# Moving the narrow t1 products of a two-layer graph kernel from behind the first attention unit to the front of the joined product

## The chip, the cores and the metric

The kernel runs on one core of one Trainium2 chip. The metric is the time of one execution on the device in microseconds (us), smaller being better. All data is 32-bit floating point.

## What is computed

Two layers run over 16 batch elements of 1024 nodes with 256 channels. Layer 0 weights the shared adjacency by a likeness of nodes, derives queries from it, and does attention with 4 heads; layer 1 is a pair of graph convolutions with the same adjacency. The core of the reference:

```
def layer0(x, para, adj, kv_w):          # x: 16 x 1024 x 256
    fea = transpose(x, (0, 2, 1))
    c_adj = mean(fea, axis=1)
    diff = c_adj[:, None, :] - c_adj[:, :, None]
    A = abs(abs(sigmoid(diff) - 0.5) - 0.5) * 2.0
    Wg = adj[None] * (A + transpose(A, (0, 2, 1))) * 0.5
    g = relu(einsum('bcn,bnm->bcm', fea, Wg) * para.reshape(1, C, N))
    q = heads(transpose(g, (0, 2, 1)))
    k, v = heads(x @ kv_w)
    attn = softmax(einsum('bhnd,bhmd->bhnm', q, k) * scale)
    return merge(einsum('bhnm,bhmd->bhnd', attn, v))

def graph_conv(x, adj, w_loop, w_neigh, b):
    return x @ w_loop + einsum('nm,bmh->bnh', adj, x @ w_neigh) + b

x = layernorm(x + layer0(x, para, adj, kv_w))
h = relu(graph_conv(x, adj, w1_loop, w1_neigh, b1))      # 256 -> 128
h = relu(graph_conv(h, adj, w2_loop, w2_neigh, b2))      # 128 -> 256
x = layernorm(x + (x + h) * 0.5)
```

`t1` in the kernel is `x @ w1_neigh` of the first convolution, a 1024 x 128 array.

## The kernel before

The batch elements are software-pipelined. While element b is in attention, the next element's query weights, keys and values are prepared (`q`, `kv`), the first convolution of element b-1 (`c1`) and the second convolution of element b-2 (`c2`) are done together, and element b-3 (`c3`) gets its last normalization.

**Attention in four units.** `UNITS` are four pairs of (heads, half of the queries). For each unit u, `Attention.scores(u)` (L618) makes 8 score tiles with products on half of TensorE's rows (64 x 128 weights, two products side by side, L626); ACT takes the exponential of each (L629) and VectorE sums them up (L633, L635), transposes the sum (L637) and reduces it (L640). `Attention.outputs(u)` (L643) multiplies the exponentials with the values, on half of TensorE's columns (L648), and VectorE transposes the result (L653). Between units the main loop (L1095 to L1122) calls one of three functions: `gap0` behind unit 0, `gap1` behind unit 1, `gap2` behind unit 2. `gap0` and `gap1` run for b = 1 to 14; `both`, the joined product, exists from b = 2 on.

**The t1 products.** `GraphConv.inner` (L750) makes t1 with 16 products of 128 columns (L755) into a PSUM tile of two banks and has ACT copy it to SBUF (L758, 128 x 1024). The group has 32 entries in a trace for each call: every 32-bit product is recorded as two passes.

**The joined product.** The first convolution of b-1 and the second of b-2 both multiply by the adjacency. `Joined` treats the pair as one blocked product with 7 in place of 8 block products (a Strassen form). Its left-hand sums of t1 and of the second convolution's h1 are made by `Joined.left` (L924) with four 128 x 512 additions, on GpSimd within the loop and on VectorE at the very end. Its right-hand sums of the adjacency lie in DRAM and are fetched by `Joined.fetch` (L920, DMA at L183). `Joined.run` (L942) starts with the loop products of `c1` (`GraphConv.loop`, L760; they use x and not t1), then takes products 1, 2, 6, 7, 5, 4 and 3 through `Joined.product` (L935), each of 4 products of 512 columns. Products 1 and 2 use t1 itself as weights; 6 uses `s12[:, 1]`, 7 `s34[:, 0]`, 5 `s12[:, 0]`, 3 `s34[:, 1]` and 4 h1. Into this sequence `gap1` hangs other work: the GpSimd sums for the next query (`FastQueries.left`, L534, behind product 1), the accumulation of the attention (`att.add`, L655, behind product 2), the likenesses (L490, L491), the last normalization of `c3` and more. The last batch element (L1178 to L1189) and the end of the kernel (L1191 to L1205) have their own order, in which `c1.inner()` and `both.left(...)` stand directly ahead of `both.run(...)`.

**What sets the order.** The whole program is under a manual schedule: each engine runs its instructions in the order of the Python calls, and waits are put in from the data dependencies and the buffers. SBUF rows (`row_tile`) come from a ring of 25 buffers, taken in the order of first use; a tile waits for the last readers of the tile 25 places earlier. PSUM has a ring of three two-bank tiles (`big_psum`, `half_psum`), which serves the scores, t1, the joined product's sums and the second convolution's outputs (`h2_ps`, L838, read by VectorE at L830), and a ring of two single banks. SyncE (SP) issues all DMAs of the loop in program order.

Of the kernel before, what the change touches and what calls it, by code (L numbers as in the profile page):

```python
# [18 lines left out]
def kernel(  # L19
# [31 lines left out]
    nc = tc.nc  # L51
# [47 lines left out]
    def row_tile(name):  # L99
        return work.tile([P, N], F32, tag="row", name=name, bufs=ROWS)  # L100
# [85 lines left out]
    def store(n, rows):  # L186
        for h in range(2):
            nc.sync.dma_start(out=far_adj[n][h], in_=rows[h])
# [7 lines left out]
    def adj_sums(rows01, k):  # L196

        w11, w21, w22 = (half_adj[ij][:, k, :] for ij in ((0, 0), (1, 0), (1, 1)))
        w12 = of_rows(rows01, k)
        t13, t24 = (row_tile(f"adjT_{n}_{k}") for n in (13, 24))  # L200
        t = {1: t13[:, 0:FB], 3: t13[:, FB:N], 2: t24[:, 0:FB], 4: t24[:, FB:N]}
        nc.vector.tensor_sub(t[1], w12, w11)
        nc.vector.tensor_sub(t[3], w22, w12)
        nc.vector.tensor_sub(t[2], w22, t[1])
        nc.vector.tensor_sub(t[4], w21, t[2])
        for n in t:
            nc.sync.dma_start(out=far_adj[n][k // 2][:, ts(k % 2, FB)], in_=t[n])
# [9 lines left out]
    def channel_major(blocked, name):  # L217

        dst = work.tile([P, NC, N], F32, tag="xT", name=name, bufs=2)
        for cc in range(NC):  # L220
            nc.vector.transpose(dst[:, cc, :], blocked[cc])
        return dst
# [35 lines left out]
    def means(q, xb, name):  # L258

        c_col = small.tile([P, NT], F32, tag="c_col", name=f"c_col_{name}", bufs=2)  # L260
        for t in range(NT):
            nc.scalar.activation(xb[:, t, :], xb[:, t, :], AF.Identity, accum_out=c_col[:, t:t + 1])
        nc.gpsimd.tensor_scalar_mul(c_col, c_col, 1.0 / C)
        line = dram.tile([1, N], F32, tag="line", name=f"line_{name}")
        nc.sync.dma_start(out=line.rearrange("o (t p) -> p (o t)", p=P), in_=c_col)
        q.c_col = c_col

        def row():
            q.c_row = work.tile([P, N], F32, tag="c_row", name=f"c_row_{name}")
            nc.sync.dma_start(out=q.c_row, in_=line.to_broadcast([P, N]))  # L270

        return row
# [241 lines left out]
    class FastQueries(Queries):  # L514
# [19 lines left out]
        def left(self, eng):  # L534
            s12, s34 = (row_tile(f"S_{self.b}_{k}").rearrange("p (s t c) -> p s t c", s=2, c=P) for k in range(2))
            eng.tensor_add(s12[:, 0], self.block(1, 0), self.block(1, 1))
            eng.tensor_sub(s12[:, 1], s12[:, 0], self.block(0, 0))
            eng.tensor_sub(s34[:, 0], self.block(0, 0), self.block(1, 0))
            eng.tensor_sub(s34[:, 1], self.block(0, 1), s12[:, 1])
            self.S = [s12[:, 0], s12[:, 1], s34[:, 0], s34[:, 1]]  # L540
# [366 lines left out]
    class Joined:  # L907
# [16 lines left out]
        def left(self, eng):  # L924

            t1 = [self.c1.t1[:, j * TJ:(j + 1) * TJ, :] for j in range(2)]
            h1 = [self.c2.h1[:, ts(j, FB)].rearrange("p (t f) -> p t f", f=HID) for j in range(2)]
            s12, s34 = (row_tile(f"R_{self.b}_{k}").rearrange("p (s t f) -> p s t f", s=2, f=HID) for k in range(2))
            eng.tensor_add(s12[:, 0], h1[0], h1[1])
            eng.tensor_sub(s34[:, 0], t1[0], h1[0])  # L930
            eng.tensor_sub(s12[:, 1], s12[:, 0], t1[0])
            eng.tensor_sub(s34[:, 1], t1[1], s12[:, 1])
            self.x = {1: t1[0], 2: t1[1], 3: s34[:, 1], 4: h1[1], 5: s12[:, 0], 6: s12[:, 1], 7: s34[:, 0]}

# [45 lines left out]
    def run():  # L980
# [57 lines left out]
        for b in range(B):  # L1038
            more = b + 1 < B
            att = Attention(b, xB, qT, kT, v)  # L1040
            c1, c2, c3 = (convs.get(b - k) for k in (1, 2, 3))
            both = Joined(c1, c2) if c2 else None
# [9 lines left out]

            def gap0():
                row = means(q, xb, str(b + 1))
                c1.inner()
                if both:
                    c2.load_x()
                    both.fetch(2, 3)
                    both.left(nc.gpsimd)
                row()  # L1060
                ready["xT"] = channel_major(blocked, f"xT_{b + 1}")

            def weigh_first():
                q.times_adj(0)
                q.times_adj(TJ)
                q.right(0)

            def gap1():
                for t in (0, TJ):
                    q.load(t)  # L1070
                if both:
                    both.fetch(1, 4)
                    both.run({1: (lambda: q.left(nc.gpsimd),),
                              2: (lambda: att.add(0, 1),),
                              6: (lambda: q.likeness(0), lambda: c3 and c3.moments()),
                              7: (lambda: q.likeness(TJ),),
                              5: (weigh_first,),
                              4: (lambda: c3 and c3.finish(out[b - 3]),),
                              3: (c1.turn_blocks,)})
                else:  # L1080
                    q.left(nc.gpsimd)
                    for t in (0, TJ):
                        q.likeness(t)
                    store("01", rows01)
                    c1.first(rows01, lambda: (att.add(1), adj_sums(rows01, 1), adj_sums(rows01, 2), weigh_first()))
                    c1.turn_blocks()

            def gap2():
                if both:
                    c2.last()  # L1090

            between = [gap0, gap1, gap2] if c1 and more else []
            if more:
                q = (FastQueries if c1 else Queries)(b + 1, xb)
# [96 lines left out]
        c1, c2, c3, c4 = (convs[B - k] for k in (1, 2, 3, 4))  # L1191
        both = Joined(c1, c2)
# [83 lines left out]
```

## Time and profile before

| | us |
|---|---|
| median of 3 runs | 2154.06 (2153.91 to 2154.83) |
| the profiled execution | 2154.23 |
| its span, first to last instruction | 2152.5 |
| t1 products, L755, busy in all 16 calls | 61.3 |
| t1 copies, L758, ACT, in all 16 calls | 16.2 |
| R sums, L929 to L932, GpSimd, 14 calls each | 21.7, 21.3, 21.7, 29.4 |

The granted TensorE clock was 0.998 over the span. How to read the page: "PE" is TensorE's products, "PEld" its loads of weights, "DVE" VectorE, "POOL" GpSimd; a line such as L755 is the line of the program that issued an instruction. In a timeline, each row gives the start of a group in us from the span's start, its length, the engine, the line, the operation, output and inputs, the shapes, and the number of instructions merged; in brackets stands the idle time of the engine ahead of it and what ended it. A pair such as 64\*128 or 128\*64 in the shapes is the part of the array that a product uses.

### The profile page before, as it was taken

The numbers are of one execution on the slowest core, as the hardware profiler recorded it, in microseconds if no ns is written. First come the engines' busy times: TensorE is split into PE (matmuls) and PEld (weight loads), VectorE is DVE, ScalarE is ACT, GpSimd is POOL, SyncE is SP. The second block draws the span as 40 slices with busy tenths as digits, with TensorE's granted clock in tenths as the row PEclk, the third lists the DMA queues.
The fourth block names the chain that finished last, engine by engine and source line by source line (L and its number), as shares of the span: only waits on it lengthen the run. The fifth ranks groups of instructions, "written<-read, shape, count | busy, mean of one in ns | idle before, by whom it ended". The sixth has DMA issues, their size and how long they took to land.

```text
span 2152.5 us, 23740 instructions
## 1 busy us (share of the span) xinstructions
PE 2138.9 (99%) x8360; PEld 1023.1 (48%) x8360; DVE 1905.3 (89%) x2350; ACT 1039.9 (48%) x1374; POOL 361.1 (17%) x201
## 2 busy tenths in 40 slices
PE   9999999999999999999999999999999999999998
PEld 5344444544445444454545445454454444544354
DVE  5999998899998999989999899999999899899964
ACT  4744545545345454455544555445553445545412
POOL 1011130211303113030120302203021130211021
PEclk9999999999999999999999999999999999999999
DMA  9493563736557365572755627555374563734343
GB/s 231 120 150 117 141 163 108 142 122 131 143 140 168 93 134 158 135 171 89 122 165 129 161 89 121 173 127 157 108 114 160 128 157 119 130 133 95 121 137 100
DMA packets 612207, 290.73 MB, mean 135 GB/s; under 512 B 504816, under 2 KB 569712, under 8 KB 612080
## 3 DMA queue, kind: packets, MB, share of 16 engines
q1 hardware_dynamic: 611808, 288.87, 55.7%
q8 instruction: 68, 1.11, 0.2%
q14 instruction: 59, 0.48, 0.1%
q10 hardware_dynamic: 272, 0.26, 0.0%
HBM read 242.35 MB, written 46.72 MB: 134 GB/s over the span
## 4 chain that ended last, share of the span: by engine, by line


## 5 line engine op out<-in xcount | busy, mean ns | idle before, releaser
L629 ACT ACTIVATE pr<-s 128x1024 f32<-128x1024 f32 x512 | 476.1, 1054 | 175.1 <-PE s L626 174.3
L635 DVE TENSOR_TENSOR acc<-acc,pr 128x1024 f32<-128x1024 f32 x384 | 492.7, 1283 | 42.2 <-DVE acc L635 2.4
L626 PE MATMUL s<-qT,kT 64*128 64x512 f32 x2048 | 456.8, 596 | 0.0
L648 PE MATMUL av<-pr,v 128*64 128x512 f32 x2048 | 453.6, 596 | 0.0
L626 PEld LDWEIGHTS s<-qT,kT 64*128 64x128 f32 x2048 | 191.7, 186 | 236.6 <-ACT pr L629 112.3
L328 POOL TENSOR_TENSOR rstd<-rstd,neg_half 128x32 f32<-128x32 f32 x16 | 98.9, 6182 | 1113.8 <-DVE rstd L326 1113.8
L648 PEld LDWEIGHTS av<-pr,v 128*64 128x64 f32 x2048 | 141.4, 137 | 298.6 <-issue 292.1
L490 ACT ACTIVATE wg<-c_row,c_col 128x1024 f32<-128x1024 f32 x128 | 146.1, 1141 | 76.4 <-DVE accB L637 65.7
L496 DVE SCALAR_TENSOR_TENSOR wg<-wg,adj 128x1024 f32<-128x1024 f32 x128 | 150.0, 1210 | 11.4 <-ACT wg L491 11.1
L939 PE MATMUL hu_ps<-adj,R 128*128 128x512 f32 x360 | 158.0, 595 | 0.0
L491 ACT ACTIVATE wg<-wg 128x1024 f32<-128x1024 f32 x128 | 135.3, 1057 | 4.1
L577 PE MATMUL g_ps<-wg,S 128*128 128x512 f32 x224 | 115.6, 598 | 0.0
L577 PE MATMUL g_ps<-T,S 128*128 128x512 f32 x224 | 115.2, 596 | 0.0
L577 PE MATMUL g_ps<-wg,x 128*128 128x512 f32 x224 | 109.0, 599 | 0.0
L633 DVE TENSOR_TENSOR acc<-pr,pr 128x1024 f32<-128x1024 f32 x64 | 80.5, 1258 | 30.0 <-ACT pr L629 30.0
L939 PE MATMUL hu_ps<-adjT,t 128*128 128x512 f32 x240 | 105.7, 593 | 0.0
L939 PEld LDWEIGHTS hu_ps<-adj,R 128*128 128x128 f32 x360 | 67.4, 190 | 78.8 <-issue 77.2
L586 ACT COPY P<-g_ps 128x512 f32<-128x512 f32 x14 | 8.2, 585 | 174.8 <-PE g_ps L577 174.8
L637 DVE STREAM_TRANSPOSE accB<-acc 128x1024 f32<-128x1024 f32 x64 | 79.7, 1245 | 2.2
L955 ACT COPY snap<-hu_ps 128x512 f32<-128x512 f32 x15 | 8.8, 585 | 150.3 <-PE hu_ps L939 150.3
L640 DVE TENSOR_REDUCE den_part<-accB 128x32 f32<-128x1024 f32 x64 | 78.1, 1220 | 2.2
L823 PE MATMUL h_ps<-w2n_sb,uT 128*128 128x256 f32 x240 | 72.8, 385 | 0.0
(204 smaller groups left out, 3020.6 us busy)
## 6 DMA issues: line engine op xcount, KB each, us to landing
adj<-in_adj_dram SPq DMA_DIRECT2D x128, 512.0 KB, 5.0
adj<-adjT SPq DMA_DIRECT2D x120, 512.0 KB, 10.1
para<-in_L_gnn_para_dram SPq DMA_DIRECT2D x32, 512.0 KB, 4.5
xB_a<-in_x_dram SPq DMA_DIRECT2D x128, 128.0 KB, 3.9
x1d<-xB_a SPq DMA_DIRECT2D x128, 128.0 KB, 3.4
x<-x1d SPq DMA_DIRECT2D x16, 1024.0 KB, 16.1
xB<-in_x_dram SPq DMA_DIRECT2D x120, 128.0 KB, 4.7
x<-in_x_dram SPq DMA_DIRECT2D x15, 1024.0 KB, 6.5
```

Of the source, the lines that this page charges most:

```text
L328: nc.gpsimd.tensor_tensor(self.rstd, self.rstd, neg_half, ALU.pow)
L490: nc.scalar.activation(wg, self.c_row, AF.Abs, bias=self.c_col[:, t:t + 1], scale=-1.0)
L491: nc.scalar.activation(wg, wg, AF.Tanh, scale=-0.5)
L496: nc.vector.scalar_tensor_tensor(wg, wg, 1.0, self.adj.pop(t), op0=ALU.add, op1=ALU.mult)
L577: nc.tensor.matmul(self.p[n], x_n[:, k, :], w_n, start=(k == 0), stop=(k == TJ - 1))
L626: nc.tensor.matmul(ps[:, ts(s, FB)], self.kT[rows, pair, ts(mt, P)], self.qT[rows, pair, ts(j, FB)], start=True, stop=True)
L629: nc.scalar.activation(pr, ps, AF.Exp)
L633: nc.vector.tensor_add(acc, self.pr[0], pr)
L635: nc.vector.tensor_add(acc, acc, pr)
L637: nc.vector.transpose(accB, acc)
L648: nc.tensor.matmul(pav[s * HD:(s + 1) * HD, :], self.v[:, mt, pair * P + s * HD:pair * P + (s + 1) * HD], self.pr[mt][:, ts(s, FB)], start ...
L939: nc.tensor.matmul(dst, self.x[n][:, k, :], half_adj[w][:, k, :] if w else of_rows(rows, k), start=(start and k == 0), stop=(k == TJ - 1), ...
```

## The change

In `gap0`, the call of `c1.inner()` and the four sums of `both.left(nc.gpsimd)` are taken out. In `gap1`, `c1.inner()` is put behind the two adjacency loads and, where there is a joined product, `both.left(nc.gpsimd)` behind it, both ahead of the fetch of adjacency sums 1 and 4 and of `both.run`. In b = 1, which has no joined product, `c1.inner()` then stands ahead of `q.left(nc.gpsimd)`, the likenesses and `c1.first`. In `Joined.left` the second and third of the four sums change places, so that `s12[:, 1]` is made ahead of `s34[:, 0]`; this holds wherever the helper is used.

```
             eng.tensor_add(s12[:, 0], h1[0], h1[1])
+            eng.tensor_sub(s12[:, 1], s12[:, 0], t1[0])
             eng.tensor_sub(s34[:, 0], t1[0], h1[0])
-            eng.tensor_sub(s12[:, 1], s12[:, 0], t1[0])
             eng.tensor_sub(s34[:, 1], t1[1], s12[:, 1])
...
             def gap0():
                 row = means(q, xb, str(b + 1))
-                c1.inner()
                 if both:
                     c2.load_x()
                     both.fetch(2, 3)
-                    both.left(nc.gpsimd)
                 row()
                 ready["xT"] = channel_major(blocked, f"xT_{b + 1}")
...
             def gap1():
                 for t in (0, TJ):
                     q.load(t)
+                c1.inner()
                 if both:
+                    both.left(nc.gpsimd)
                     both.fetch(1, 4)
                     both.run({1: (lambda: q.left(nc.gpsimd),),
```

The number of instructions of each engine's arithmetic is the same before and after: TensorE runs scores of unit 1 directly behind outputs of unit 0, and t1 between outputs of unit 1 and the loop products; ACT runs the t1 copy behind unit 1's exponentials in place of ahead of them; GpSimd keeps its order apart from the swap, and SyncE keeps its order of DMAs.

More of the change, by code (lines that the diff above doesn't have):

```diff
@@ L929, in left @@
             eng.tensor_add(s12[:, 0], h1[0], h1[1])
+            eng.tensor_sub(s12[:, 1], s12[:, 0], t1[0])
             eng.tensor_sub(s34[:, 0], t1[0], h1[0])
-            eng.tensor_sub(s12[:, 1], s12[:, 0], t1[0])
             eng.tensor_sub(s34[:, 1], t1[1], s12[:, 1])
@@ L1054, in gap0 @@
                 row = means(q, xb, str(b + 1))
-                c1.inner()
                 if both:
@@ L1058, in gap0 @@
                     both.fetch(2, 3)
-                    both.left(nc.gpsimd)
                 row()
@@ L1070, in gap1 @@
                     q.load(t)
+                c1.inner()
                 if both:
+                    both.left(nc.gpsimd)
                     both.fetch(1, 4)
```

## The prediction

> **What bounds the kernel now.** I read the busy times first, then TensorE's timeline around the place of the edit, then the same stretch on the other engines.
>
> ```profile
> PE   2138.9 (99%) x8360; PEld 1023.1 (48%) x8360; DVE 1905.3 (89%) x2350; ACT 1039.9 (48%) x1374; POOL 361.1 (17%) x201
> ```
>
> TensorE (PE) is busy for 2138.9 of 2152.5 us. A busy share can hide stalls, so I checked the starts: the loop products that open a joined product (L762) start 132.34 us apart in every batch element from the second joined one on (561.26, then 693.60; 958.28, then 1090.63). An interval that repeats this exactly waits for nothing; the time is the sum of TensorE's own blocks. A change can only shorten a block, or bring in a wait that is not there now.
>
> The blocks around the edit, from TensorE's timeline (start, length, group). Lengths include the pipeline's tail, so I use differences of starts.
>
> ```profile
> 1065.76 7.09 PE L648 MATMUL av<-pr,v 128*64 128x512 f32 x32
> 1072.77 3.84 PE L755 MATMUL t_ps<-w1n_sb,x1T 128*128 128x128 f32 x32
> 1076.54 7.14 PE L626 MATMUL s<-qT,kT 64*128 64x512 f32 x32
> 1083.61 7.09 PE L648 MATMUL av<-pr,v 128*64 128x512 f32 x32
> 1090.63 1.98 PE L762 MATMUL hu_ps<-x1T,w1l_sb 128*128 128x512 f32 x4
> 1092.45 7.03 PE L939 MATMUL hu_ps<-adjT,t 128*128 128x512 f32 x16
> ```
>
> The reader should see four changes of array shape: 128*64 (outputs) to the full array (t1), to 64*128 (scores), to 128*64, to the full array (loop). Steps: outputs 7.01, t1 3.77, scores 7.07, outputs 7.02, loop 1.82.
>
> The new order is already in the trace, at the last batch element, where the inner product stands right before the joined one, and where scores follow outputs with nothing between:
>
> ```profile
> 1992.14 7.09 PE L648 MATMUL av<-pr,v 128*64 128x512 f32 x32
> 1999.16 7.14 PE L626 MATMUL s<-qT,kT 64*128 64x512 f32 x32
> 2006.23 0.41 PE L662 MATMUL den_ps<-den_part,fold 128*128 128x32 f32 x2
> ...
> 2042.43 3.84 PE L755 MATMUL t_ps<-w1n_sb,x1T 128*128 128x128 f32 x32
> 2046.11 1.88 PE L762 MATMUL hu_ps<-x1T,w1l_sb 128*128 128x512 f32 x4
> 2047.83 3.60 PE L939 MATMUL hu_ps<-adjT,t 128*128 128x512 f32 x8
> ```
>
> Here outputs to scores is 7.02, scores 7.07, t1 followed by loop 3.68, loop after t1 1.72.
>
> **What the Trainium skill says.** "TensorEngine Tiling (Array Packing)", Tiling Modes, Key Properties: "Changing tiling mode (not just tile) drains the TensorE". It gives no price; the trace agrees and prices it: the same loop block is 1.82 behind outputs and 1.72 behind t1. "TensorE: Matmul & The Clock Gate", Step-by-step: the weights of a coming product are loaded while the present one runs. The weight loads of L762 and L939 agree (each starts some 0.43 ahead of its product). "SBUF — State Buffer", Who interferes with whom: a VectorE instruction with two SBUF inputs and a GpSimd instruction that reads SBUF exclude each other. The trace agrees: L387 of VectorE takes 1.75 beside GpSimd's S sums, while L386, of the same shape, takes 0.68.
>
> **The change part by part.**
>
> *TensorE.* No product is added or removed; 16 t1 products (32 recorded passes) move in 14 batch elements (b = 1 to 14; the last element and the ending have the order already). Per element:
> - t1 is followed by the full-array loop in place of scores: 3.77 − 3.68 = 0.09 saved.
> - The loop follows t1 in place of outputs: 1.82 − 1.72 = 0.10 saved.
> - Outputs to scores without t1 between: 7.02 against 7.01, and scores then take 7.07 as before: nothing.
> - Scores to outputs stays: nothing.
>
> Sum 0.19 us by 14 = 2.7 us, all on the path, since TensorE is the path. Two changes of shape fall away of four. The saving's own bounds are rounding of starts: 0.18 to 0.20 by 14, so 2.5 to 2.8.
>
> *ACT.* The t1 copy (L758, 1.01) moves from before the eight exponentials of unit 1 to behind them. They now follow the means (L262), which end at about 1070.45, before scores could start at 1072.8. So neither delays scores, and the copy finds ACT idle: ACT's exponentials end about 8.6 after their scores start, while outputs end 14.1 after. Cover on the new side: product 1 needs t1's copy for its weights, and only the loop (1.72) lies between. In the last element:
>
> ```profile
> 2046.31 1.01 ACT L758 COPY t<-t_ps 128x1024 f32<-128x1024 f32 x1 [9.68 <-PE t_ps L755]
> 2047.40 0.19 PEld L939 LDWEIGHTS hu_ps<-adjT,t 128*128 128x128 f32 x1 [0.24 <-ACT t L758]
> ```
>
> The copy ends at 2047.32, the weight load starts at 2047.40 in its usual rhythm, the product at 2047.83: 0.43 behind the load that takes 0.19, so 0.08 plus 0.24 = 0.3 us of cover. Uncovered, every tenth over it would cost 1.4 us in all. I take 0; bounds 0 and 0.1 each (1.4), not below nothing since the product can't precede its weights.
>
> *GpSimd.* The four R sums (1.27 each alone, 1.6 to 2.25 beside VectorE) move behind the t1 copy, and what is queued behind them is the four S sums of the next query (L536 to L539), now later by the R sums. The swap in the helper lets the sum for product 6 come first: ready at loop start + 1.24 + at most 2.3 = 3.5. Product 6 starts 8.86 after loop start (1099.48). R for product 7 follows by 5.8, needed at 12.3; the last by 8, needed at 24. S is first used in the next query's steps, after unit 3. Cost 0.
>
> *SyncE and buffers.* No DMA is moved in its queue. The row buffers are a ring of 25, and t1 and the two R rows are taken behind the adjacency rows of the gap: rows between take a buffer whose last user is three places older. The program shows one fresh wait that could matter: the third exponential of unit 1 now waits for the normalized rows' stores (L341). They have landed 19 to 24 us before loop start, that exponential runs some 15 before it: 4 us of cover. Adjacency loads wait for older, earlier users. The sums of the gap no longer stand between. Cost 0.
>
> *VectorE* is the one to watch. It loses contention in unit 1's sums and finds it later. With L386 to L389 three instructions contend either way, with R now, with S before. S then runs from about 6.3 to at most 13 after loop start, and meets L672 and L674 (two SBUF inputs, 0.69 now, from 10.3 on). The trace doesn't show these contended; by L387 each costs between 0 and 1.75 − 0.68 = 1.07. I take one or two: VectorE 1.1 to 2.1 late. Its slack:
>
> ```profile
> 1119.34 1.25 DVE L784 STREAM_TRANSPOSE h1B<-h1T 128x1024 f32<-128x1024 f32 x1 [0.53 <-ACT h1T L768]
> 1121.66 1.22 DVE L633 TENSOR_TENSOR acc<-pr,pr 128x1024 f32<-128x1024 f32 x1 [1.07 <-ACT pr L629]
> ...
> 1139.81 1.22 DVE L830 TENSOR_TENSOR z<-h_ps,b_sb 128x1024 f32<-128x1024 f32 x1 [0.97 <-PE h_ps L825]
> ```
>
> 0.53 + 1.07 + 0.97 = 2.57 us, then the residual sum (L830) frees a PSUM buffer late for unit 3's third score tile. Below 2.57 the path pays nothing. The element at 561.26 is a natural trial: contention left it 1.5 late there (its L633 starts at 592.53 without any idle), and TensorE's next loop start came 132.34 later all the same.
>
> **Total.** Against the profiled execution: span 2152.5 − 2.7 = 2149.8, plus the 1.7 around it, 2151.5. That execution took 2154.23, 0.17 above the median of 2154.06; against the median, 2154.06 − 2.7 = **2151.4**.
>
> **Rivals.**
> - *The saving is given back* (no change, 2154.0): a drain at the new edge costs what the old two did. For it: the skill has no price, and the savings are tenths. Against: the last element shows the new edges themselves, and all others are constant to 0.01. Also here: the weight load of product 1 slips by 0.1 to 0.2 in each element, giving 1.4 to 2.8 back: 2152.8 to 2154.2.
> - *VectorE falls behind* (slower): all seven GpSimd sums run at the contended 1.7, from 1.2 to 13.3 after loop start, and four two-input instructions (two each of L672 and L674) contend: 4 × 1.07 = 4.3, less 2.57 is 1.7 us of stall before unit 3's scores, in the 13 elements with a joined product: 22 us, so 2154.1 − 2.7 + 22 = 2173. It decides from 2.57 us of lateness on. Against it: VectorE's earlier start (it loses 1.3 us less in unit 1's sums, idles before L958) and S sums that run uncontended at 1.27 under transposes and PSUM reads.
> - *More than that* (2149 or less): would need over 0.31 us an element, yet TensorE's products stay the same and only two changes of shape go. Next to nothing.
>
> **How the numbers follow.** Forecast 0.79, within 2150.7 to 2152.1. Saving given back, whole or part: 0.13, 2152.1 to 2154.6. VectorE behind: 0.06, 2157 to 2173. Bigger gain: 0.02. The range 2150.4 to 2153.8 takes the forecast and most of the second case. A measurement of this kernel can tell about 0.2% (4.3 us) from no change; the forecast's gain, 0.13%, is below that. Faster by over 0.2%: 0.02; within: 0.92; slower: 0.06.
>
> **What would show it.** In the profile after: the loop starts 132.15 apart; t1 to loop 3.68 and loop to product 1 1.72 in all elements; no idle of the weight loader on the t1 copy above 0.24; the R sums start about 1.3 behind loop start; L672 or L674 longer than 0.69, the idle before L784 and L633 shrunk or gone, that before L830 still above 0. Wrong if the interval grows, with an idle of unit 3's score weights on L830, or if the loop block stays at 1.82.

## The result and the profile after

| | before, us | after, us |
|---|---|---|
| median (range, runs) | 2153.94 (2152.97 to 2154.93, 18) | 2150.33 (2149.86 to 2151.23, 18) |
| the profiled execution | 2154.23 | 2150.00 |
| its span | 2152.5 | 2148.2 |
| interval between the loop products (L762) of neighbouring batch elements, joined elements | 132.34 | 132.15 |

The ratio is 0.9984, with a 95% interval of 0.9977 to 0.999: a gain of 3.6 us. That is below the 0.2% that the prediction gave as the least to be told from no change, though the interval excludes 1.

The busy times of after:

```profile
PE 2136.2 (99%) x8360; PEld 1021.5 (48%) x8360; DVE 1906.8 (89%) x2350; ACT 1039.8 (48%) x1374; POOL 355.2 (17%) x201
```

The instruction counts are the same; TensorE's busy time is 2.7 us less, and VectorE's 1.5 us more. TensorE's last products start 3.9 us earlier (2141.59 before, 2137.70 after); where do these come from? TensorE's timeline of after in a middle element:

```profile
1070.25 7.14 PE L626 MATMUL s<-qT,kT 64*128 64x512 f32 x32
1077.32 7.09 PE L648 MATMUL av<-pr,v 128*64 128x512 f32 x32
1084.34 3.84 PE L755 MATMUL t_ps<-w1n_sb,x1T 128*128 128x128 f32 x32
1088.01 1.88 PE L762 MATMUL hu_ps<-x1T,w1l_sb 128*128 128x512 f32 x4
1089.73 7.03 PE L939 MATMUL hu_ps<-adjT,t 128*128 128x512 f32 x16
```

Take differences of starts: scores 7.07, outputs 7.02, t1 3.67, loop 1.72. In the trace of before, t1 took 3.77 and the loop 1.82. No row has an idle time in brackets: TensorE waits for nothing here. The loop starts are 132.15 apart in each of 12 intervals between joined elements, as constant as the 132.34 of before.

What fell away can be counted. Between two loop starts the array shape in TensorE's records changes 12 times in before and 11 times in after. Outputs to t1, t1 to scores, scores to outputs and outputs to the loop were four changes; outputs to scores, scores to outputs and outputs to t1 are three. The one change that the move created, outputs straight to scores, shows the price. Here are neighbouring products of after at that place, and the first load of weights for the scores:

```profile
1069.29 0.60 PE L648 MATMUL av<-pr,v 128*64 128x512 f32 x2
1069.72 0.60 PE L648 MATMUL av<-pr,v 128*64 128x512 f32 x2
1070.25 0.70 PE L626 MATMUL s<-qT,kT 64*128 64x512 f32 x2
1070.79 0.60 PE L626 MATMUL s<-qT,kT 64*128 64x512 f32 x2
1071.21 0.60 PE L626 MATMUL s<-qT,kT 64*128 64x512 f32 x2
```

```profile
1070.25 0.19 PEld L626 LDWEIGHTS s<-qT,kT 64*128 64x128 f32 x2 [0.81 <-PE av L648]
```

Within a block the products start 0.43 apart. Across the change it is 0.53, and behind it 0.53 once more (0.54 in the rounded starts): 0.10 in the last product ahead and 0.10 in the first one behind, 0.20 in all. The load starts together with its product, where inside a block it runs 0.43 ahead. The same sum over all changes of before gives 0.20 for outputs to t1, outputs to the loop, outputs to scores and any full-array block to scores, and 0.12 to 0.15 for changes into outputs. So the move takes away one change of about 0.20 in each of 14 elements, 194 to 180 in the whole program, which accounts for the difference between 132.34 and 132.15.

The copy of t1, and the first load of weights that needs it:

```profile
1088.21 1.01 ACT L758 COPY t<-t_ps 128x1024 f32<-128x1024 f32 x1 [9.35 <-PE t_ps L755]
1089.30 0.19 PEld L939 LDWEIGHTS hu_ps<-adjT,t 128*128 128x128 f32 x1 [0.24 <-ACT t L758]
```

The copy ends at 1089.22 and the load starts at 1089.30, 0.43 ahead of its product, in the rhythm of all loads. The idle time of 0.24 that the trace puts down to the copy is the loader's usual pause: loads that wait for nothing show the same 0.24.

GpSimd's timeline, same element:

```profile
1076.86 2.11 POOL L929 TENSOR_TENSOR R<-h 128x512 f32<-128x512 f32 x1 [8.11 <-DVE xT L221]
1089.37 1.59 POOL L930 TENSOR_TENSOR R<-R,t 128x512 f32<-128x512 f32 x1 [10.39 <-DVE den_part L640]
1090.92 1.71 POOL L931 TENSOR_TENSOR R<-t,h 128x512 f32<-128x512 f32 x1
1092.59 1.71 POOL L932 TENSOR_TENSOR R<-t,R 128x512 f32<-128x512 f32 x1
...
1098.50 1.72 POOL L539 TENSOR_TENSOR S<-x,S 128x512 f32<-128x512 f32 x1
```

The first R sum needs only h1 and runs during unit 1, ahead of t1. So three sums, and not four, run behind the copy, from 1.36 us after loop start to 6.3; the S sums follow from 6.25 to 12.2. (The releaser in L930's bracket is inferred and misleads. L930 reads t1, whose copy ends at 1089.22, 0.02 ahead of L640; in all joined elements it starts 0.14 behind the copy, also in those where L640 was long done.)

VectorE beside the last S sum, and then further on in the same element:

```profile
1098.22 0.87 DVE L672 TENSOR_TENSOR o<-o,rden 128x512 f32<-128x512 f32 x1
1099.12 1.64 DVE L674 TENSOR_TENSOR xB_a<-xB_a,o 128x512 f32<-128x512 f32 x1
...
1101.40 0.68 DVE L672 TENSOR_TENSOR o<-o,rden 128x512 f32<-128x512 f32 x1
1102.12 0.69 DVE L674 TENSOR_TENSOR xB_a<-xB_a,o 128x512 f32<-128x512 f32 x1
```

```profile
1113.94 0.69 DVE L972 TENSOR_TENSOR uT<-snap,hu_ps 128x512 f32<-128x512 f32 x1
...
1117.13 1.23 DVE L784 STREAM_TRANSPOSE h1B<-h1T 128x1024 f32<-128x1024 f32 x1
1118.95 1.23 DVE L633 TENSOR_TENSOR acc<-pr,pr 128x1024 f32<-128x1024 f32 x1 [0.58 <-ACT pr L629]
...
1137.09 1.22 DVE L830 TENSOR_TENSOR z<-h_ps,b_sb 128x1024 f32<-128x1024 f32 x1 [0.97 <-PE h_ps L825]
```

The L674 that runs beside GpSimd takes 1.64, the next one 0.69. L672 takes 0.18 more; the two together, 0.95 + 0.18, less 0.10 by which VectorE arrives earlier at L672 (10.21 after loop start, 10.31 before), make VectorE 1.0 us late from there on (L277 starts 15.43 after loop start, 14.41 before). The lateness is paid from idle time: ahead of L784 0.53 goes to 0, ahead of L633 1.07 goes to 0.58, and ahead of L830 the 0.97 is whole again. Over the whole run the groups of after show the exchange, here by line with busy time and the mean in ns:

```profile
L635 DVE TENSOR_TENSOR acc<-acc,pr 128x1024 f32<-128x1024 f32 x384 | 482.9, 1258 | 42.2 <-DVE acc L635 2.8
L674 DVE TENSOR_TENSOR xB_a<-xB_a,o 128x512 f32<-128x512 f32 x64 | 54.7, 855 | 2.3
```

L674 grew from 44.3 to 54.7 us in all, L635 shrank from 492.7 to 482.9: the contention moved from unit 1's sums to the joined product.

**The part of the gain that the change of order does not explain.** The starts account for the profiled pair as follows. From the first product of the keys (L352) to TensorE's last product, after is 2.73 us shorter: 2133.13 before (8.46 to 2141.59), 2130.40 after (7.30 to 2137.70). The start of L352 itself is 1.16 earlier, and from TensorE's last product to the end of the span there is 0.3 less. TensorE's timeline at the very start, first of before, then of after:

```profile
7.96 0.66 PE L232 MATMUL xT_ps<-ident,x 128*128 128x128 f32 x4 [1.00 <-DMA x<-in_x_dram]
8.46 1.88 PE L352 MATMUL k_ps<-xT,kvw_sb 128*128 128x512 f32 x4
```

```profile
4.86 2.60 PE L232 MATMUL xT_ps<-ident,x 128*128 128x128 f32 x16
7.30 3.17 PE L352 MATMUL k_ps<-xT,kvw_sb 128*128 128x512 f32 x7
```

The loads of weights for these transposes (L232) waited for x by 0.51, 0.32 and 1.24 in before, by 0.34 and 0.35 in after. The change touches no instruction there. This is looked at again with the experiments.

### The profile page after: what moved, and what is told of

It is laid out like the page before. It is cut to its first block, busy times and chain, and to the rows that moved or that the text cites. A ratio compares the mean times of both kernels' runs of the same rounds, so it can differ in the third digit from the quotient of the medians.

```text
span 2148.2 us, 23745 instructions
## 1 busy us (share of the span) xinstructions
PE 2136.2 (99%) x8360; PEld 1021.5 (48%) x8360; DVE 1906.8 (89%) x2350; ACT 1039.8 (48%) x1374; POOL 355.2 (17%) x201
## 4 chain that ended last, share of the span: by engine, by line
## 5 line engine op out<-in xcount | busy, mean ns | idle before, releaser
L635 DVE TENSOR_TENSOR acc<-acc,pr 128x1024 f32<-128x1024 f32 x384 | 482.9, 1258 | 42.2 <-DVE acc L635 2.8
L633 DVE TENSOR_TENSOR acc<-pr,pr 128x1024 f32<-128x1024 f32 x64 | 77.0, 1203 | 19.7 <-ACT pr L629 19.7
L758 ACT COPY t<-t_ps 128x1024 f32<-128x1024 f32 x16 | 16.2, 1013 | 143.9 <-PE t_ps L755 143.9
L640 DVE TENSOR_REDUCE den_part<-accB 128x32 f32<-128x1024 f32 x64 | 78.0, 1220 | 2.2
L823 PE MATMUL h_ps<-w2n_sb,uT 128*128 128x256 f32 x240 | 72.7, 385 | 0.0
```

The costliest lines, as they stand in the source:

```text
L635: nc.vector.tensor_add(acc, acc, pr)
L640: nc.vector.tensor_reduce(self.part[:, u % 2, :], by_node(accB), AX.X, ALU.add)
```

## The experiments

Seven kernels. Beside them the kernel before was measured on the same chip: 2153.48 for the first four, 2153.63 for move_only, 2153.82 for the last two. The last column counts the changes of array shape between two loop starts.

| kernel | median, us (runs) | ratio to before, 95% interval | interval, us | changes of shape |
|---|---|---|---|---|
| swap_only | 2152.95 (13) | 0.9998, 0.999 to 1.0007 | 132.34 | 12 |
| split_t1 | 2152.62 (13) | 0.9996, 0.9987 to 1.0004 | 132.34 | 12 |
| last_joined | 2146.90 (6) | 0.9969, 0.9957 to 0.9982 | 131.95 | 10 |
| loop_first | 2167.89 (5) | 1.0067, 1.0054 to 1.0081 | 133.51 | 11 |
| move_only | 2150.09 (21) | 0.9984, 0.9978 to 0.9991 | 132.15 | 11 |
| dve_late2 | 2150.90 (20) | 0.9986, 0.9979 to 0.9993 | 132.15 | 11 |
| dve_late4 | 2162.97 (5) | 1.0042, 1.0027 to 1.0056 | 133.1 | 11 |

### The swap alone (swap_only)

The kernel before, with only the second and third R sums exchanged.

```
-            eng.tensor_sub(s34[:, 0], t1[0], h1[0])
             eng.tensor_sub(s12[:, 1], s12[:, 0], t1[0])
+            eng.tensor_sub(s34[:, 0], t1[0], h1[0])
```

> The kernel before with only the second and third R sum exchanged; t1 stays behind unit 0. TensorE's blocks keep their order. Theory (the gain is two changes of array shape fewer): same as before, 2153.9, loop starts 132.34 apart. Rival (the part of the measured gain beyond 2.7 us, 0.9 us, comes from the order of the sums): about 2153.0.

Measured: 2152.95, interval 132.34. The swap gives nothing inside the loop. This run also bears on the start of the program: its L352 starts at 7.51, 0.95 ahead of that of before, and the loop of its last batch element at 2045.17, 0.94 ahead of 2046.11. From the first product of the keys on, swap_only and before are the same program in time, so nearly a microsecond of difference between profiled executions can come from the start alone, here from when x landed. Against swap_only, after is 2.62 us faster by the medians (2152.95 − 2150.33, from different groups of runs), or 3.1 if each is first compared with the before measured beside it; the traces say 2.73.

### The move alone (move_only)

After, with the R sums in the old order.

```
-            eng.tensor_sub(s12[:, 1], s12[:, 0], t1[0])
             eng.tensor_sub(s34[:, 0], t1[0], h1[0])
+            eng.tensor_sub(s12[:, 1], s12[:, 0], t1[0])
```

> The kernel after with the R sums in the order of before, so that the sum for product 6 comes third and not second. Theory (GpSimd has cover: ready at about 6.3 us after loop start, product 6 starts 8.75 after): no difference to the kernel after, interval 132.15, 2150.3. Rival (the exchange is what keeps product 6 from waiting): some tenths of a us in each of 13 elements, 2153 or more.

Measured: 2150.09, interval 132.15, as after. Its sum for product 6 (L931 here) ends at 1092.63 by GpSimd's timeline, 4.6 us after loop start, and product 6 starts 8.8 after it. The swap wasn't needed: the move alone gives the whole effect on the interval.

### Half of t1 on each side (split_t1)

After, with t1 in two halves of 8 products: the first in `gap0`, the second in `gap1`. Each half takes one bank of a two-bank PSUM tile and has its own copy on ACT, of half the size.

```
                 row = means(q, xb, str(b + 1))
+                c1.inner_half(0)
                 if both:
...
                     q.load(t)
-                c1.inner()
+                c1.inner_half(1)
```

> The kernel after, but the first half of t1 (8 products and their copy) stands behind unit 0 again and only the second half at the front of the joined product. Theory (a run of full-array products between blocks on half the array costs 0.19 us, however long it is): the four changes of shape are back, loop starts 132.34 apart, 2.7 us over the kernel after, 2153.0. Rival (what is saved goes with the products moved): half of it, interval 132.25, 1.35 us over the kernel after, 2151.7.

TensorE's timeline of split_t1 (L759 is t1, L777 the loop here):

```profile
1064.65 7.09 PE L648 MATMUL av<-pr,v 128*64 128x512 f32 x32
1071.67 2.05 PE L759 MATMUL t_ps<-w1n_sb,x1T 128*128 128x128 f32 x16
1073.65 7.14 PE L626 MATMUL s<-qT,kT 64*128 64x512 f32 x32
1080.71 7.09 PE L648 MATMUL av<-pr,v 128*64 128x512 f32 x32
1087.73 2.05 PE L759 MATMUL t1b_ps<-w1n_sb,x1T 128*128 128x128 f32 x16
1089.62 1.88 PE L777 MATMUL hu_ps<-x1T,w1l_sb 128*128 128x512 f32 x4
```

The half between tiled blocks takes 1.98 (1071.67 to 1073.65), the half ahead of the loop 1.89. Together 3.87, which is 0.10 more than the undivided block of before (3.77) and 0.20 more than that of after. The interval is 132.34, that of before: moving half of the products gave back nothing at all. The cost belongs to the changes of shape, four again at this place as in before, and not to the number of products moved.

### One more visit taken away (last_joined)

After, with the second convolution's last products (`c2.last`, L823 and L825, full array) moved from between unit 2 and unit 3 to directly behind the joined product.

```
                               3: (c1.turn_blocks,)})
+                    c2.last()
...
             def gap2():
-                if both:
-                    c2.last()
+                pass
```

> The kernel after, with the second convolution's outer products (L823, L825) moved from between units 2 and 3 to directly behind the joined product, so that one run of full-array products less stands between the units. Theory: 0.19 us less in each of 13 elements, interval 131.95, 2.5 us under the kernel after, 2147.8. Rival (VectorE: the residual sums now stand in front of unit 2's sums, and the outer products wait for the last sum L972): up to 1 us more in each element, 2163.

TensorE's timeline of last_joined; 14 rows of L823 and L825 between are left out:

```profile
1110.94 3.60 PE L939 MATMUL hu_ps<-adjT,R 128*128 128x512 f32 x8
1114.37 0.59 PE L823 MATMUL h_ps<-w2n_sb,uT 128*128 128x256 f32 x2
...
1120.85 0.59 PE L825 MATMUL h_ps<-w2l_sb,h1T 128*128 128x256 f32 x2
1121.37 4.13 PE L626 MATMUL s<-qT,kT 64*128 64x512 f32 x18
```

The products now follow the joined product in the same shape, and the scores of unit 2 come behind them. Outputs to full array and full array to scores, two changes, became one, outputs to scores. Interval 131.95, another 0.20 less in each of 13 elements, or 2.6 us; the span is 3.1 us below that of after. At 0.9969 of before (0.9957 to 0.9982) this is the fastest kernel of the study: its slowest run (2147.32) is below the fastest of after (2149.86, from another group of runs), though the two ratio intervals overlap by 0.0005. VectorE is not hurt: ahead of L830 it still has 0.97 of idle time.

### The cover of the t1 copy taken away (loop_first)

After, with the loop products ahead of t1, so that nothing lies between t1 and product 1.

```
             c1.loop(third, 0, start=True)
+            turn_to(0)
             self.product(1, first, start=True)
...
-                    both.left(nc.gpsimd)
                     both.fetch(1, 4)
-                    both.run({1: (lambda: q.left(nc.gpsimd),),
+                    both.run({0: (c1.inner, lambda: both.left(nc.gpsimd)),
+                              1: (lambda: q.left(nc.gpsimd),),
```

> The kernel after, with the loop products put ahead of t1 where there is a joined product, so that nothing stands between t1 and product 1. Theory (the loop hides t1's copy, 1.01 us, and its waits): product 1 waits about 1.2 us in 13 elements, interval 133.3, 15 to 16 us over the kernel after, 2166. Rival (the copy of the first half would have been in time anyway, since the wait is only for what is read): 0, 2150.3.

TensorE and then ACT of loop_first, the latter with its waiting time ahead:

```profile
1093.37 1.98 PE L762 MATMUL hu_ps<-x1T,w1l_sb 128*128 128x512 f32 x4
1095.19 3.73 PE L755 MATMUL t_ps<-w1n_sb,x1T 128*128 128x128 f32 x32
1100.03 7.13 PE L939 MATMUL hu_ps<-adjT,t 128*128 128x512 f32 x16 [1.10 <-ACT t L758]
```

```profile
1098.96 1.01 ACT L758 COPY t<-t_ps 128x1024 f32<-128x1024 f32 x1 [11.06 <-PE t_ps L755]
```

The copy ends at 1099.97, product 1 starts at 1100.03. The interval is 133.51, which is 1.36 above after: of the loop's 1.72, 1.36 had been hiding the copy, and the rest was cover left over (0.36 by this, 0.32 by the starts of after). Over 13 elements that makes 17.7, and the medians differ by 17.6. So the order inside the joined product, t1 and then the loop, is what hides the copy.

### VectorE made late (dve_late2, dve_late4)

After, with a subtraction of 128 x 512 (that of L552, which writes the same values again) repeated two or four times at the end of `weigh_first`, in joined elements. Each takes 0.72. (A first form, dve_plus2 and dve_plus4, with transposes into a spare tile, has no time: the tile found no room in SBUF.)

```
                 q.right(0)
+                if both:
+                    t12, t4 = q.T[0]
+                    for _ in range(4):
+                        nc.vector.tensor_sub(t4, q.wg[TJ][:, 0:FB], t12[:, FB:N])
```

> The kernel after, with VectorE's subtraction L552 made three times in place of once in the joined product (the same result written again; about 0.72 us each), so that VectorE is some 1.45 us later ahead of the sum L972. Theory (slack left in the kernel after: 0.58 ahead of unit 2's first sum L633 and 0.97 ahead of the second residual sum L830, 1.55 together): it just fits, interval 132.15, 2150.3. Rival (any further lateness of VectorE reaches TensorE): up to 1.45 us in each of 13 elements, 2169.

> The same with the subtraction made five times, about 2.9 us later. Theory (slack 1.55, then the second residual sum L830 frees a PSUM buffer late and unit 3's third score tile waits): about 1.3 us of stall in each of 13 elements, interval about 133.5, 2167. Rival (VectorE catches up elsewhere, or the slack is larger than read): interval 132.15, 2150.3.

With two, the interval stays at 132.15 and the idle time ahead of the second L830 shrinks but does not vanish. VectorE of dve_late2:

```profile
1137.32 1.22 DVE L830 TENSOR_TENSOR z<-h_ps,b_sb 128x1024 f32<-128x1024 f32 x1 [0.39 <-PE h_ps L825]
```

With four, the interval is 133.1, 0.94 more, in ten of twelve; one is 133.55, and the first stays at 132.15, where L972 starts 26.5 us after loop start and not 28.8. The kernel is slower than before. The waits of TensorE in dve_late4, summed up (us in all, times, the longest), and the place in one element:

```profile
PE s L626 <- DVE uT L972: 8.4, 12, 1.1
```

```profile
1121.29 1.13 PE L626 MATMUL s<-qT,kT 64*128 64x512 f32 x4
1123.09 6.28 PE L626 MATMUL s<-qT,kT 64*128 64x512 f32 x28 [0.67 <-DVE uT L972]
1143.42 7.14 PE L626 MATMUL s<-qT,kT 64*128 64x512 f32 x32
```

```profile
1122.35 0.69 DVE L972 TENSOR_TENSOR uT<-snap,hu_ps 128x512 f32<-128x512 f32 x1
...
1143.56 1.22 DVE L830 TENSOR_TENSOR z<-h_ps,b_sb 128x1024 f32<-128x1024 f32 x1
```

The stall that the slow rival feared exists, but it stands elsewhere: in the scores of unit 2 behind the first tile, where the next tile's PSUM buffer is still being read by L972 (the last reader of the joined product's sums), and not in unit 3 behind L830. Unit 3's scores (1143.42) run through without a wait, although L830 has lost all its idle time; but TensorE had been held for nearly as long as L830 was late, so how much later L830 may come was hardly tested. In this element the loop starts at 1093.50, so L972 ends 29.54 after loop start; in after it ends at 1114.63, 26.62 behind 1088.01. It was thus 2.9 late (4 times 0.72), TensorE was held for 0.94, and so the slack of after at L972 is 2.0 us. dve_late2 is 1.4 late there, inside that slack, and it did not stall.

## Why the prediction was right, point by point

- **The saving and its size held; the count of changes did not.** 3.67 and 1.72 came out against the forecast 3.68 and 1.72. The traces shorten by 2.73 us between L352 and the last products against the 2.7 forecast. But "Two changes of shape fall away of four" is one too many: outputs directly followed by scores is a change too, and three of the four remain. The sum did not suffer, because its terms 0.09 and 0.10 are measured steps, and they were the two halves of one change of 0.20, not two changes of 0.10. What was only inferred from the last element is now shown: where TensorE is not held up, the interval follows the changes of shape, 132.34 with 12 (before, swap_only, split_t1), 132.15 with 11 (after, move_only, dve_late2), 131.95 with 10 (last_joined).
- **"An interval that repeats this exactly waits for nothing" is not safe.** loop_first repeats at 133.51 just as exactly, with a wait of 1.1 us in each joined element. That before had nothing to wait for rests on its trace: TensorE's products have no recorded wait behind the first load of x.
- **"Changing tiling mode drains".** The Trainium skill ("TensorEngine Tiling (Array Packing)", Tiling Modes, Key Properties) says that the switch drains TensorE. The trace agrees: at a change the next product starts 0.10 late, and its weights are loaded with it and not ahead. So the forecast's "each starts some 0.43 ahead of its product" does not hold for the first product behind a change; in before the first load of L762 starts at 1090.62, its product at 1090.63.
- **The time itself, 2151.4, was 1.1 us too high** (2150.33, just below the range's lower end of 2150.4). Part of this is the reference: before measured 2153.94 here and not 2154.06. The gain by the medians is 3.6, not 2.7, and the excess of 0.9 is of the size of what differs at the start: L352 starts at 8.46 (before), 7.51 (swap_only), 7.36 (split_t1), 7.30 (after, move_only), 7.16 (last_joined), 8.14 (loop_first), 7.52 (dve_late2) and 8.07 (dve_late4). Two things vary there: when x lands, and until when the first products start 0.21 apart in place of 0.11 (4.5 in before, 7.0 in dve_late4). These are single profiled executions, and whether a kernel keeps its start over many runs wasn't measured. swap_only and split_t1, with the interval of before, also came out 0.5 and 0.9 below the before beside them, though their ratio intervals include 1. So that the excess comes from the start is argued, not shown; that it isn't the loop is shown by the starts.
- **The t1 copy was covered,** by 0.32 as forecast (0.3); loop_first measured what the loop was hiding, 1.36 for each element.
- **GpSimd came earlier than bounded.** "The four R sums move behind the t1 copy" was wrong by one: L929 doesn't read t1. R for product 6 was ready 2.95 after loop start (bound 3.5), for product 7 by 4.6 (5.8), the last by 6.3 (8), and S ended at 12.2 (13). VectorE's lateness came out just below its forecast, 1.0 against 1.1 to 2.1: one L674 and a part of one L672 contended, with 0.95 and 0.18 against the bound of 1.07 each. This agrees with the Trainium skill's "SBUF — State Buffer", Who interferes with whom, by which a VectorE instruction with two SBUF inputs contends with a GpSimd instruction that reads SBUF: L674 took 1.64 beside L539 and 0.69 without a GpSimd sum.
- **The idle times went as forecast:** ahead of L784 gone, ahead of L633 halved, ahead of L830 untouched.
- **The slow rival had the place wrong.** "0.53 + 1.07 + 0.97 = 2.57 us" is the slack up to L830. The path is held at L972, over 20 us earlier. After is already 1.0 late there (25.93 after loop start, 24.91 in before) and has 2.0 left, so the slack of before at L972 was about 3.0. The forecast did not look for another PSUM buffer that TensorE needs sooner. At 1.0 us of lateness both bounds leave room, so the number wasn't hurt. By the measured slack, the rival's 4.3 us would have cost 4.3 − 3.0 = 1.3 us in each element in place of its 1.7. The natural trial was stronger than "1.5 late": in the element at 561.26, L972 starts 26.91 after loop start, 2.0 later than in most others, and TensorE was not held.
- **The rival "saving given back" falls** with the interval of after. The new edge, outputs to scores, does cost 0.20, but t1 between them had cost that twice.

## What to carry to other kernels

On an engine that is always busy, compare the length of the same block behind different neighbours; a difference between its starts is a cost of the order alone. Then count the changes of array shape and price one from the starts of single products, since two whole blocks can look alike when both pay. The cost can be had back by grouping blocks of one array shape, as last_joined shows by doing it once more. When a moved step gets a new cover for its copy, test that cover by taking it away. For an engine that comes late, look for the earliest deadline among the buffers that it frees, not for the one that the profile's idle time points to.

## What was not expected of the hardware

Going from outputs straight to scores, from one half-array shape to the other, costs as much as going from outputs to the full array or from the full array to scores: 0.20. The block steps hide this: outputs (128\*64) took 7.02 whether the full array or scores (64\*128) followed, and scores took 7.07 behind the full array as behind outputs, which looks like a free change. The single products show 0.10 at the end of outputs and 0.10 at the start of scores in either case. The price falls in two near halves on the two blocks that meet: t1 took 3.67 with full-array products next and 3.77 with scores next, so 0.09 to 0.10 on leaving; the loop took 1.82 behind outputs and 1.72 behind t1, so 0.10 on entering. It did not depend on how many products a block has (8 or 16 in split_t1). Why changes into outputs cost less (0.12 to 0.15) was not looked into.
